# Graph network of four layers on one core: when a group's norms, roots, bounds and skip products are issued in layers 1 and 2

## The chip, the core and the metric

The kernel runs on one core of a Trainium2 chip. The metric is device time of one execution in microseconds (us); the time before is 1505.42 us, the median of three runs (1503.63 to 1510.78). The core has five engines that run beside each other, each with its own queue of instructions: TensorE (PE in the profile, its weight loads PEld), VectorE (DVE), ScalarE (ACT), GpSimd (POOL) and SyncE (SP), which here only issues DMA transfers. [...]

## What is computed

A graph of 3125 nodes with 128 features and 103125 edges goes through four layers; after each, the layer's output is added to its input and normalized over the 128 features.

```python
x = _layernorm(x + _L0_gnn_ref(...))   # weighted sum over edges, weight matrix, relu
x = _layernorm(x + _L1_gnn_ref(...))   # attention with 4 heads, and a norm of its own
x = _layernorm(x + _L2_gnn_ref(...))   # attention with one head, Q, K, V, Wo
x = _layernorm(x + _L3_gnn_ref(...))   # two mean aggregations, sigmoid
```

Layer 1 is the one that the change touches most. Its output for a node is

```python
out = sum over edges of alpha * h[src]         # alpha: softmax of leaky_relu(a_s[src] + a_d[dst])
out = out + gat_bias + x @ skip_W + skip_b
out = (out - mu) * rsqrt(var + 1e-5) * ln_g + ln_b
```

so two norms follow each other: the layer's own one, with its scale `ln_g` and shift `ln_b`, and then, with the layer's input added, the one around the layer.

## The kernel before

Nodes are padded to 25 blocks of 128. The first third of the run turns the edge list into dense count and weight matrices in DRAM. The attention of layers 1 and 2 and the sums of layer 3 are then matmuls over these matrices, with one accumulator bank in PSUM for each block of target nodes.

**Layer 1** goes over four groups of target blocks (`IG`: blocks 0 to 5, 6 to 12, 13 to 18 and 19 to 24, called groups 0 to 3 here), for each over two pairs of heads (`hp`), and for each pair over the 25 source blocks `c`. One (group, pair, c) is an *item*, 200 in all. For an item, `masks` loads a block of counts (`ct`) and makes two bf16 masks `cm`: of five masks, four come from an ACT instruction (`fm`, L1286) and a DVE one (L1287), and one from a single longer DVE instruction (L1280). `products` then issues three matmuls for each target block (L1297, L1302). Masks are made two items ahead of the products that use them. After a pair's 25 items, `sums` reads the accumulators on DVE (L1321) and combines them on POOL (L1327 to L1332); `quotients` divides and adds the result to `r` (L1337 to L1343). `r` already holds the skip product, which `skips` computes one block an item, a matmul into a spare bank (L1310) and a DVE addition (L1311).

**What follows a group.** When both pairs of heads of a group are summed, `finish1` runs its end beside the next group's items, as a chain of steps. `first_norm` takes the moments on DVE (`norm1`: L1021, L1023, L1025) and the square root on ACT (L1026). `first_scale` finishes the reciprocal on DVE and scales each block on ACT (`norm2`: L1031 to L1035), and then POOL multiplies by `ln_g`, adds `ln_b` and adds the input (L1082 to L1084). `second_norm` and `second_scale` do the same once more, into `x`. `turns` then takes the blocks one by one, two items each: `turn2` transposes the block on PE (L1044), copies it to `xT` (L537 on ACT or L539 on DVE, in turn), multiplies it for layer 2 (L1048), squares it on ACT (L1049) and copies a part to `vo` on DVE (L1050). When a half of the blocks (`QG`: 13 and 12) has been turned, `bound2` finds an upper bound for the exponents of layer 2: a maximum on DVE (L1058), `highest` (a transpose on PE, L1002, and DVE, L1004 to L1007), and an item later `spread` (PE, L1013) and a square root on ACT (L1064).

**Layer 2** goes over the two halves (`q`) and the 25 source blocks: 50 items more. `scores` makes an item's scores on PE (L1445) in banks of a pool of three (`ss`), exponentials on ACT (L1448) and a product with the counts on DVE (L1449); `products2` multiplies with `vo` (L1453). The end of layer 1's last group runs in layer 2's first items, and takes its spare banks from the same pool of three. `degrees` computes one over each node's degree for layer 3: on DVE, then a transpose on PE into such a bank (L1423), a copy on ACT (`rt`, L1425) and two DMAs.

**The order of the work.** The steps above are put off by `later(k, f)`: `f` is called at the beginning of the item that lies `k` items on (`step`). That is the order in which the program is written. The framework's scheduler then decides the order in each engine's queue: it may bring an instruction forward past others that it takes to be not ready yet, or put it back. On the chip each engine takes its queue in order, so that an instruction that waits holds all behind it. In the built program the queue of DVE around a second norm, and not the number given to `later`, says between which masks its moments stand.

Of the kernel before, what the change touches and what calls it, by code (L numbers as in the profile page):

```python
# [10 lines left out]
AF = mybir.ActivationFunctionType  # L11
# [18 lines left out]
H, C = 4, 32  # L30
# [472 lines left out]
IG = [(0, 6), (6, 7), (13, 6), (19, 6)]  # L503
# [7 lines left out]
def fast_path(  # L511
# [473 lines left out]
    def later(k, f):  # L985
        due.append((now[0] + k, f))
# [12 lines left out]
    def highest(sp, v, n):  # L999

        t = bank()
        nc.tensor.transpose(t[0:n, 0:P], v, ident)  # L1002
        m = sp.tile([P, 1], F32, name="m_all")
        nc.vector.memset(m, 0.0)  # L1004
        nc.vector.tensor_reduce(m[0:n, :], t[0:n, 0:P], AX.X, OP.max)
        d = sp.tile([P, 2 * H], F32, name="d_all")[:, 0:n]
        nc.vector.tensor_scalar(d, ident[:, 0:n], m[:, 0:1], None, OP.mult)  # L1007
        return d
# [7 lines left out]
    def norm1(sp, i, i0, n):  # L1016

        bs = sp.tile([P, 13, 6], F32, name="bs1")[:, 0:n]
        mv = sp.tile([P, 13, 2], F32, name="mv1")[:, 0:n]
        for b in range(n):  # L1020
            nc.vector.bn_stats(bs[:, b, :], i[:, i0 + b, :])  # L1021
        for b in range(n):
            nc.vector.bn_aggr(mv[:, b, :], bs[:, b, :])  # L1023
        sd = sp.tile([P, 13], F32, name="sd1")[:, 0:n]
        nc.vector.tensor_scalar(sd, mv[:, :, 1], EPS, None, OP.add)  # L1025
        nc.scalar.activation(sd, sd, AF.Sqrt)  # L1026
        return sp, mv, sd

    def norm2(state, o, i, i0, n):
        sp, mv, sd = state  # L1030
# [23 lines left out]
    def bound2(sp, q):  # L1054

        i0, n = QG[q]
        mq = sp.tile([P, 1], F32, name="mq")
        nc.vector.tensor_reduce(mq, nq[:, i0 : i0 + n], AX.X, OP.max)  # L1058
        d = highest(sp, mq, 1)

        def rest():
            mm = sp.tile([P, 1], F32, name="mm")
            spread(d, 1, mm)
            nc.scalar.activation(mm, mm, AF.Sqrt)  # L1064
            nc.vector.tensor_scalar(nm[:, q : q + 1], mm, -1.0001, None, OP.mult)

        later(1, rest)

    def finish1(sp, g, gap):

        i0, n = IG[g]
        rs = r[:, i0 : i0 + n, :]
        xs = x[:, i0 : i0 + n, :]
        keep = {}

        def first_norm():
            keep["a"] = norm1(sp, r, i0, n)
            later(gap[0], first_scale)

        def first_scale():  # L1080
            norm2(keep["a"], r, r, i0, n)
            nc.gpsimd.tensor_tensor(rs, rs, g_row[:, None, :].to_broadcast([P, n, P]), OP.mult)  # L1082
            nc.gpsimd.tensor_tensor(rs, rs, b_row[:, None, :].to_broadcast([P, n, P]), OP.add)
            nc.gpsimd.tensor_tensor(rs, rs, xs, OP.add)  # L1084
            later(gap[1], second_norm)

        def second_norm():
            keep["b"] = norm1(sp, r, i0, n)
            later(gap[0], second_scale)

        def second_scale():
            norm2(keep["b"], x, r, i0, n)
            nc.gpsimd.memset(vo[:, i0 : i0 + n, P : P + 1], 1.0)
            later(gap[0], lambda: turns(0))

        def turns(j):
            if j < n:
                one, two = turn2(sp, i0 + j)
                one()
                later(1, two)  # L1100
                later(2, lambda: turns(j + 1))
            else:
                nc.gpsimd.tensor_tensor(xs, xs, xs, OP.add)
                for q, (a, m) in enumerate(QG):
                    if i0 < a + m <= i0 + n:
                        later(1, lambda q=q: bound2(sp, q))

        first_norm()

    with ExitStack() as st:  # L1110
# [204 lines left out]
        def sums(acc, g, hp):  # L1315

            i0, n = IG[g]
            pool = lp if (g, hp) == (len(IG) - 1, H - 2) else sp
            nz = pool.tile([P, 7, 2, PW], F32, name="nz")[:, 0:n]
            for k in range(n):  # L1320
                nc.vector.tensor_reduce(  # L1321
                    nz[:, k], acc[k][:, 0 : 2 * HW].rearrange("p (h s c) -> p h c s", s=3, c=PW), AX.X, OP.add
                )
            hi = nz[:, :, :, 0:F1]
            lo = nz[:, :, :, F1 : 2 * F1]
            fbb = [fb[:, s, i0 : i0 + n, hp : hp + 2, None].to_broadcast([P, n, 2, F1]) for s in range(2)]
            nc.gpsimd.tensor_tensor(lo, lo, fbb[1], OP.mult)  # L1327
            nc.gpsimd.tensor_tensor(hi, hi, fbb[0], OP.mult)
            nc.gpsimd.tensor_tensor(hi, hi, lo, OP.add)
            nc.gpsimd.tensor_tensor(hi, hi, self_[:, i0 : i0 + n, hp : hp + 2, :], OP.add)  # L1330
            if hp == 0:
                nc.gpsimd.tensor_copy(deg[:, i0 : i0 + n], nz[:, :, 0, 2 * F1])  # L1332
            last = pool is lp

            def quotients():
                rz = pool.tile([P, 7, 2], F32, name="rz")[:, 0:n]
                nc.vector.tensor_scalar(rz, hi[:, :, :, C], 1e-38, None, OP.max)  # L1337
                nc.vector.reciprocal(rz, rz)
                nc.gpsimd.tensor_tensor(
                    hi[:, :, :, 0:C], hi[:, :, :, 0:C], rz[:, :, :, None].to_broadcast([P, n, 2, C]), OP.mult  # L1340
                )
                rh = r[:, i0 : i0 + n, hp * C : (hp + 2) * C].rearrange("p b (h c) -> p b h c", c=C)
                nc.gpsimd.tensor_tensor(rh, rh, hi[:, :, :, 0:C], OP.add)  # L1343
                if hp == H - 2:
                    later(1 if last else 3, lambda: finish1(ends[-1], g, (1, 1) if last else (1, 5)))

            later(1 if last else 4 if g else 7, quotients)

# [2 lines left out]
        for x_, (g, hp, c) in enumerate(items):  # L1351
            i0, n = IG[g]
            if (g, hp, c) == (1, 0, 0):
                zero.close()
                ap = st.enter_context(tc.tile_pool(name="f_ap1", bufs=1, space=PSUM))
                turn = [0]

                def few():

                    turn[0] ^= len(acc) < 7  # L1360
                    return ap.tile([P, 512], F32, name="acc1_6" if turn[0] else "few")

                spare.append(few)
            if c == 0:
                if g == 0:
                    acc = [zps.tile([P, 512], F32, name="acc1", tag=f"acc{k}") for k in (3, 4, 2)]
                    acc += [zpp.tile([P, 512], F32, name="acc1", tag=k) for k in ("tr_sa", "left0", "left1")]
                else:
                    acc = [ap.tile([P, 512], F32, name=f"acc1_{k}") for k in range(n)]
            if c == (2 if g else 0) and hp == (0 if g else H - 2):  # L1370
                later(0, lambda: skips(i0, i0 + n))
            if (g, hp, c) == (0, 2, 5):
                later(0, in_range)
            step()
            if g == 0 and hp == 0 and ready < NB and ready <= c + 4:
                values(ready)
                ready += 2
            for y_ in range(x_ if x_ == 0 else x_ + 2, min(x_ + 3, len(items))):
                masks(*items[y_])
            if c < NB - 2:  # L1380
                for k in range(n):
                    products(acc, g, hp, c, k)
            elif c == NB - 1:
                for k in range(n):
                    products(acc, g, hp, NB - 2, k)
                    products(acc, g, hp, NB - 1, k)
                sums(acc, g, hp)
# [15 lines left out]
    with ExitStack() as st:  # L1403
# [55 lines left out]
        def finish2(q):  # L1459

            i0, n = QG[q]
            halves = [(i0, n // 2), (i0 + n // 2, n - n // 2)]
            keep = {}

            def one(h):
                keep[h] = norm1(ends[-1], r, *halves[h])
                later(1, lambda: two(h))

            def two(h):
                norm2(keep[h], x, r, *halves[h])  # L1470
                if h == 0:
                    later(1, lambda: one(1))
                elif q == 0:
                    for g in range(3):
                        later(1 + g, lambda g=g: ips.update({g: in_parts(cp, g, x[:, 4 * g : 4 * g + 4, :])}))

            if q == 0:
                later(1, lambda: one(0))
            else:
                layer_norm(l2, x, r, QG[q])  # L1480
# [5 lines left out]
        for x_, (q, c) in enumerate(items):  # L1486
# [1 line left out]
            if c == 0:  # L1488
                acc = [ap.tile([P, 512], F32, name=f"acc2_{k}") for k in range((n + 2) // 3)]
            step()  # L1490
            if (q, c) == (0, 3):
                degrees()
            if (q, c) == (1, 12):
                for b in range(2):
# [290 lines left out]
```

## Time and profile before

The profiled execution took 1509.73 us, its span 1507.9 us; the median of the three runs is 1505.42 us. PE is busy for 92% of the span. A busy PE is not PE at its pace, since matmuls are pipelined and their ends modelled; so the number of matmuls that start in a stretch is read as well.

| stretch, us | stage | PE busy | DVE busy | ACT busy | POOL busy | granted clock |
|---|---|---|---|---|---|---|
| 541 to 950 | layer 1, items | 369.76 of 409 | 348.18 | 321.99 | 94.22 | 0.97 |
| 640 to 746 | items of group 1, end of group 0 | 95.96 of 106 | 86.93 | 82.00 | 25.01 | 0.98 |
| 746 to 848 | items of group 2, end of group 1 | 89.26 of 102 | 85.65 | 76.96 | 24.46 | 0.97 |
| 848 to 946 | items of group 3, end of group 2 | 91.19 of 98 | 81.67 | 72.38 | 25.00 | 0.97 |
| 950 to 1232 | layer 2, items | 277.50 of 282 | 128.86 | 142.29 | 15.80 | 0.99 |

The granted clock is the share of TensorE's full clock that the chip let through. "Idle before" in the views of the profile is time in which an engine had nothing running, and the name behind it says what ended that time.

### The profile page before, as it was taken

Reading aid. Unit: us, or ns where it says so; the run is one execution under the profiler, and the core shown is the slowest. Engines: PE = TensorE matmul, PEld = TensorE weight load, DVE = VectorE, ACT = ScalarE, POOL = GpSimd, SP = SyncE. Lnnn points to the kernel's source line nnn. Section 1 sums busy time; section 2 is a strip of 40 time slices with the busy share of each in tenths; the row PEclk is TensorE's granted clock in tenths of the full one; section 3 lists DMA queues with packets and bytes.
Section 4 is the critical chain, followed back from the end, with each engine's and each line's share of the span. In section 5 each row is a group of like instructions: output and inputs, shape, how many; then the busy total and the mean of one; then the engine's idle time right before and its main releaser. Section 6 shows DMA issues by size and latency. Waiting matters only on the chain.

```text
span 1507.9 us, 35015 instructions
## 1 busy us (share of the span) xinstructions
PE 1394.0 (92%) x14762; PEld 1225.2 (81%) x14775; DVE 981.9 (65%) x1621; ACT 908.5 (60%) x1857; POOL 129.5 (9%) x164
## 2 busy tenths in 40 slices
PE   3889999999998988988979989899999999999995
PEld 3889999999998877987978989677777774458995
DVE  4989899999991389887888879544464351012006
ACT  2978789888882489877777787454465331023003
POOL 1000000000000023132032113200000000000000
PEclk8999999999999999999999999999999999999998
DMA  7378788989887733433534534332222218513641
GB/s 206 94 184 229 194 221 241 236 212 229 240 213 223 230 115 114 138 106 107 142 83 116 143 86 116 124 112 69 69 64 77 81 58 299 198 43 131 199 154 46
DMA packets 209732, 223.91 MB, mean 148 GB/s; under 512 B 72988, under 2 KB 183371, under 8 KB 209309
## 3 DMA queue, kind: packets, MB, share of 16 engines
q1 hardware_dynamic: 208780, 218.51, 50.5%
q8 instruction: 117, 1.92, 0.5%
q0 software_dynamic: 400, 1.97, 0.4%
q10 hardware_dynamic: 385, 1.11, 0.2%
q14 instruction: 50, 0.41, 0.1%
HBM read 157.19 MB, written 64.36 MB: 147 GB/s over the span
## 4 chain that ended last, share of the span: by engine, by line
PE 72%; DVE 10%; ACT 8%; DMA 5%; issue 3%; POOL 2%; SPq 0%; DVEq 0%; ACTq 0%; POOLq 0%
PE wp L919 11%; PE acc L1453 9%; PE acc L1302 9%; PE s L1445 8%; PE acc L1553 7%; PE acc L1629 6%; PE acc L820 6%; PE acc L1297 5%; PE cp L911 4%; DVE cm L1287 3%; ACT wod L882 3%; DMA cw<-wd 2%; PE left L820 2%; ACT fm L1286 1%; DVE cm L1280 1%
## 5 line engine op out<-in xcount | busy, mean ns | idle before, releaser
L1302 PE MATMUL acc<-vp,cm 128*128 128x198 bf16 x2500 | 343.3, 252 | 7.6 <-DVE cm L1287 6.5
L1297 PE MATMUL acc<-vp,ct 128*128 128x204 bf16 x1250 | 316.5, 255 | 10.2 <-DVE vp L1205 4.5
L1286 ACT ACTIVATE fm<-adr,bas 128x768 bf16<-128x768 f32 (+1 forms) x320 | 287.2, 952 | 62.2 <-DVE cm L1287 60.4
L1302 PEld LDWEIGHTS <-cm 128*128 128x128 bf16 x2500 | 235.7, 98 | 24.4 <-DVE cm L1287 8.8
L919 PE MATMUL wp<-wod,ohc 128*128 128x128 bf16 x3768 | 239.1, 220 | 6.8 <-ACT cs L924 5.0
L919 PEld LDWEIGHTS <-ohc 128*128 128x128 bf16 x3768 | 220.3, 98 | 8.3 <-issue 7.8
L876 DVE TENSOR_TENSOR wod<-ohd,w 128x4096 bf16<-128x4096 bf16 (+2 forms) x122 | 221.5, 1869 | 0.4 <-PE wp L919 0.4
L1287 DVE TENSOR_TENSOR cm<-fm,ct 128x768 bf16<-128x768 bf16 (+1 forms) x320 | 200.3, 657 | 32.1 <-PE acc L1302 16.3
L882 ACT ACTIVATE wod<-ohd,wu 128x128 bf16<-128x128 bf16 x628 | 197.9, 398 | 0.0
L1449 DVE TENSOR_TENSOR e<-e,ct 128x416 f32<-128x416 f32 (+1 forms) x175 | 108.1, 624 | 110.2 <-ACT e L1448 102.1
L1448 ACT ACTIVATE e<-s,f_nm 128x416 f32<-128x416 f32 (+1 forms) x175 | 109.5, 632 | 103.1 <-PE s L1445 95.5
L1453 PEld LDWEIGHTS acc<-self__8043,e 128*128 128x128 f32 x1250 | 148.2, 193 | 19.8 <-issue 18.9
L820 PE MATMUL acc<-f_xw,cw 128*128 128x128 f32 x1000 | 146.8, 288 | 11.1 <-DMA cw<-wd 11.1
L1453 PE MATMUL acc<-self__8043,e 128*128 128x129 f32 x1250 | 148.5, 276 | 0.0
L1445 PE MATMUL s<-yT,f_xT 128*128 128x416 f32 (+1 forms) x350 | 143.1, 545 | 4.5 <-ACT rt L1425 2.5
L820 PEld LDWEIGHTS acc<-f_xw,cw 128*128 128x128 f32 x1000 | 126.5, 196 | 11.8 <-DMA cw<-wd 11.8
L1297 PEld LDWEIGHTS <-ct 128*128 128x128 bf16 x1250 | 121.8, 98 | 4.1 <-issue 2.9
L924 ACT CAST cs<-cp 128x500 bf16<-128x500 f32 x157 | 90.6, 577 | 39.1 <-PE cp L911 39.1
L1445 PEld LDWEIGHTS s<-yT,f_xT 128*128 128x128 f32 x350 | 62.6, 192 | 55.3 <-issue 40.8
L865 DVE TENSOR_TENSOR ohd<-kd,ramp 128x4096 bf16<-128x4096 bf16 (+1 forms) x41 | 90.2, 2201 | 20.2 <-PE cp L911 18.3
L930 ACT COPY ws<-wp 128x512 f32<-128x512 f32 x157 | 90.1, 578 | 20.6 <-PE wp L919 20.3
L911 PE MATMUL cp<-ohc,ohd 128*128 128x125 bf16 x1256 | 96.0, 220 | 4.1 <-ACT ws L930 3.8
(345 smaller groups left out, 1526.3 us busy)
## 6 DMA issues: line engine op xcount, KB each, us to landing
ct<-f_ctd SPq DMA_DIRECT2D x46, 800.0 KB
wd<-ws SPq DMA_DIRECT2D x39, 896.0 KB
cw<-wd SPq DMA_DIRECT2D x50, 640.0 KB
ct<-f_ctd SPq DMA_DIRECT2D x150, 192.0 KB
f_ctd<-cs SPq DMA_DIRECT2D x20, 1000.0 KB
ct<-f_ctd SPq DMA_DIRECT2D x50, 224.0 KB
ct<-f_ctd SPq DMA_DIRECT2D x25, 416.0 KB
ct<-f_ctd SPq DMA_DIRECT2D x25, 365.2 KB
```

Source lines behind the costliest of these rows:

```text
L820: steps.append(lambda j=j, a=cw[:, j - h, :]: nc.tensor.matmul(accs[j // 4][:, j % 4, :], a, xw[:, i, :], start=False, stop=(i == NB - 1 a ...
L876: tip[s] = nc.vector.tensor_tensor(packed(f, ww), packed(ohd, ww), twos(w2[s])[:, ww], OP.mult)
L882: nc.scalar.activation(wod[2][:, BW + w, :], ohd[:, BW + w, :], AF.Copy, scale=w3[:, 1, at : at + 1])
L911: nc.tensor.matmul(cp[:, j, 0:KW], ohd[:, w, :], ohc[:, w, 0:KW], start=(j == 0 and q == 0), stop=(j == 3 and q == 1), skip_group_check=True,)
L919: made = nc.tensor.matmul(wp[:, j, :], ohc[:, w, :], wod[s][:, w, :], start=(j == 0 and q == 0 and s == 0), stop=(j == 3 and q == 1 and s ...
L1286: nc.scalar.activation(f[:, : n * P], at, AF.Relu, bias=bas[:, c, h : h + 1], scale=UP)
L1287: nc.vector.tensor_tensor(m[:, : n * P], f[:, : n * P], ct[:, : n * P], OP.min)
L1297: nc.tensor.matmul(out_(F1, PW), ct[:, k * P : (k + 1) * P], vp[:, c, hp : hp + 2, :, 2 * F1 : V1], start=(c == 0), stop=False, skip_group ...
L1302: nc.tensor.matmul(out_(0, 2 * F1)[:, j], ms[j][:, k * P : (k + 1) * P], vp[:, c, hp + j, :, 0 : 2 * F1], start=False, stop=(c == NB - 1 a ...
L1445: nc.tensor.matmul(s[:, :m], xT[:, c * P : (c + 1) * P], yT[:, i0 * P + a : i0 * P + a + m], start=True, stop=True)
L1448: nc.scalar.activation(e[:, a : a + m], s[:, :m], AF.Exp, bias=nm[:, q : q + 1], scale=scale)
L1453: nc.tensor.matmul(acc[k // 3][:, (k % 3) * (P + 1) : (k % 3 + 1) * (P + 1)], es[q, c][:, k * P : (k + 1) * P], vo[:, c, 0 : P + 1], start ...
```

## The change

In `norm1` the square root is taken out and becomes a step of its own, `root`, one or two items behind the moments. The steps of `finish1` get other distances: for groups 0 to 2 the root comes two items behind the moments and the scaling one more (before: scaling one item behind), the second moments nine items behind the first scaling (before: five), and the turns four items behind the second scaling (before: one). The last group, which ends in layer 2, gets one item more between moments and scaling. `bound2` of the first half now has three steps, three items apart; that of the second half keeps two. For groups 1 to 3 the skip products begin at the item of source block 5 and not 2. In layer 2 `degrees` moves from source block 3 to 16, and the two norms behind the first half get the separate root too. No computation is added or left out.

```diff
@@ norm1
-        nc.scalar.activation(sd, sd, AF.Sqrt)
         return sp, mv, sd
+
+    def root(state):
+        nc.scalar.activation(state[2], state[2], AF.Sqrt)
@@ bound2
-        d = highest(sp, mq, 1)
-
-        def rest():
+        wait = 1 if q else 3
+
+        def rest(d):
...
-        later(1, rest)
+        def over():
+            d = highest(sp, mq, 1)
+            later(wait, lambda: rest(d))
+
+        if q:
+            over()
+        else:
+            later(wait, over)
@@ finish1
             keep["a"] = norm1(sp, r, i0, n)
-            later(gap[0], first_scale)
+            later(gap[0], lambda: root(keep["a"]))
+            later(gap[0] + 1, first_scale)
...
             keep["b"] = norm1(sp, r, i0, n)
-            later(gap[0], second_scale)
+            later(gap[0], lambda: root(keep["b"]))
+            later(gap[0] + 1, second_scale)
...
-            later(gap[0], lambda: turns(0))
+            later(1 if g == len(IG) - 1 else 4, lambda: turns(0))
@@ sums
-                    later(1 if last else 3, lambda: finish1(ends[-1], g, (1, 1) if last else (1, 5)))
+                    later(1 if last else 3, lambda: finish1(ends[-1], g, (1, 2) if last else (2, 9)))
@@ items of layer 1
-            if c == (2 if g else 0) and hp == (0 if g else H - 2):
+            if c == (5 if g else 0) and hp == (0 if g else H - 2):
                 later(0, lambda: skips(i0, i0 + n))
@@ finish2
                 keep[h] = norm1(ends[-1], r, *halves[h])
-                later(1, lambda: two(h))
+                later(1, lambda: root(keep[h]))
+                later(2, lambda: two(h))
@@ items of layer 2
-            if (q, c) == (0, 3):
+            if (q, c) == (0, 16):
                 degrees()
```

## The prediction

> **What bounds the kernel now.** I read the page first, then in layers 1 and 2 the waits of PE, the starts of matmuls by stretch, and the timelines of the engines around the worst stretches.
>
> ```profile
> PE 1394.0 (92%) x14762; PEld 1225.2 (81%) x14775; DVE 981.9 (65%) x1621; ACT 908.5 (60%) x1857; POOL 129.5 (9%) x164
> ```
>
> PE bounds the kernel, so only time in which PE stands still or runs slowly can be won. The change touches 600 to 1240 us. The waits of PE from 640 to 950 us (us in total, times, longest):
>
> ```profile
> PE acc L1302 <- DVE cm L1287: 6.5, 6, 3.2
> PE acc L1044 <- ACT f_x L1035: 6.0, 1, 6.0
> PE few L1310 <- DVE f_xw L1311: 5.2, 5, 2.3
> PE few L1044 <- DVE self__8043 L1050: 4.8, 2, 2.5
> PE few L1002 <- DVE mq L1058: 1.5, 1, 1.5
> PE acc L1013 <- DVE d_all L1007: 1.5, 1, 1.5
> ```
>
> In order: masks that come late, the first turn waiting for the second scaling, skip products waiting for their bank, turns waiting for theirs, and the two halves of the bound. All PE waits there come to some 30 us of 310. Slow running is seen in starts by stretch (busy PE, starts, granted clock, DMA):
>
> ```profile
> 680.00:700.00 20.00, 16.64 (x156) 0.91 0.42 122
> ...
> 720.00:750.00 30.00, 30.00 (x345) 1.00 0.51 142
> ...
> 772.00:796.00 24.00, 16.29 (x157) 0.86 0.26 71
> ...
> 872.00:894.00 22.00, 17.71 (x163) 0.84 0.29 78
> ```
>
> Undisturbed, 345 matmuls start in 30 us: 0.087 us each, so an item of 18 takes 1.57 us and one of 21 takes 1.83 us. From 772 to 796 only 157 start where 276 could. Layer 2 has hardly a stall after 985 us (PE busy 277.5 of 282). The worst stretch, on DVE, POOL and ACT:
>
> ```profile
> 776.19 4.14 DVE L1287 TENSOR_TENSOR cm<-fm,ct 128x768 bf16<-128x768 bf16 x2 [1.24 <-ACT fm L1286]
> 782.31 1.46 DVE L1021 BATCH_NORM_STATS2 bs<-f_xw 128x6 f32<-128x128 f32 x7 [1.98 <-POOL f_xw L1084]
> ```
> ```profile
> 777.64 2.27 POOL L1083 TENSOR_TENSOR f_xw<-f_xw,f_b_row 128x896 f32<-128x896 f32 x1
> 779.99 2.29 POOL L1084 TENSOR_TENSOR f_xw<-f_xw,f_x 128x896 f32<-128x896 f32 x1
> ```
> ```profile
> 785.25 0.21 ACT L1026 ACTIVATE sd<-sd 128x7 f32<-128x7 f32 x1 [3.96 <-DVE sd L1025]
> ...
> 787.38 2.79 ACT L1035 ACTIVATE f_x<-f_xw,ms,sd 128x128 f32<-128x128 f32 x7
> ```
>
> ACT scales, POOL takes three operations, DVE stands 1.98 us before the second moments with the next masks queued behind them, ACT stands 3.96 us at the root with masks behind it, and PE stands until 787.9 because a transpose of the scaled `x` is next in its queue.
>
> **The bound of the first half.** Both waits lie on PE (1.5 and 1.5 us). Three items between the steps, some 4.7 us, are more than either wait. Nothing is added. Gain 2.7; ends 2 and 3.
>
> **Roots and turns.** In the built queues the turns of groups 0 to 2 stand about 20 masks (10 items) later; the root and the second scaling also stand behind more masks, and the scalings are mixed with `fm` instead of six or seven in a row (7 x 0.40 = 2.8 us in the last row above).
> - Group 1: the 6.0 us wait for `f_x` goes. What is late next is a mask. At 781.8 us DVE has finished 230 masks of this layer's count, enough for one item more on PE (1.57, to 783.4). The new DVE queue has five of the seven moments ahead of the next mask: 782.3 + 5 x 0.21 = 783.4, then masks of 0.95 and 0.5 us, so PE goes on at 784.9 and two items later is where it is at 787.9 now, or a little ahead. It gains about two items and 0.9 us: 4 us; ends 2 (masks stay late for some items) and 6.
> - Group 0: its waits for the turns' bank are 2.5 us at 689.3 (DVE's copy waits 2.29 us for ACT's square, behind 9.4 us of `fm` that the six scalings had held up) and 2.3 us at 711 (DVE's copy behind six sums, 2.98 us). The turns now start after that pair's sums. The first wait goes, with 0.8 us at 684 for `f_xT`. Of the second, 1 us comes back as late masks. Gain 4; ends 2.5 and 5.5.
> - Group 2: a wait of 0.9 us for `f_x` goes. Gain 0.9.
> - The cost: the turns of groups 1 and 2 now begin just behind the sums of a pair. For group 1 the first copy to `xT` is DVE's, behind six sums and two masks that run beside POOL (1.2 to 1.3 us each). PE meets its matmul one item after the sums, some 2.6 us before the copy is done; a late mask would take 0.7 of it anyway. Cost 1.8; ends 0 and 3. In group 2 the first copy is ACT's and hidden.
>
> **The second moments.** Nine items instead of five read like 6 us more for POOL. But the scheduler brings the moments forward: in DVE's queue those of group 1 still start behind mask 230 (seven before; five, then two between masks after), of group 2 behind mask 328 in both, of group 0 behind 128 instead of 126. So the waits for POOL stay (1.7, 2.0 and 3.6 us), and with them the 3.2 us mask wait on PE in group 2. In group 0 three `fm` (3 x 0.95 us) now stand between three and three first scalings on ACT. POOL's input is up to 2.8 us later while DVE has two masks (1.2 us) more ahead: 1.4 us lost, ends 0 and 2.8. Here the row and a rule agree on a limit and differ on the hope. Two masks took 4.14 us beside POOL, where 1.1 us is usual (0.56 each on either side). "SBUF — State Buffer", section "Who interferes with whom", of the Trainium skill says why: an operation with two SBUF inputs and a GpSimd operation that reads SBUF exclude each other whole, the second waits. So filling the 2.0 us wait before L1084's end with masks, if the moments did move, would give by plain durations 2.0/0.56 = three masks, by the rule one at most (0.6 us). I take the rule: even a real move is worth little, and I count nothing.
>
> **The skips.** Groups 1 to 3 lose 5.2 us at L1310, since each needs DVE to be some three items ahead. Three items later DVE has had about 3 x 0.4 us to recover (a mask pair costs 75% of a PE item: DVE busy is 22.6 of 30 us in 720 to 750), but the first norm's moments, 2.5 us of DVE, now stand ahead of most skips. Gain 2; ends -1 and 5.
>
> **Layer 2.** PE waits 2.54 us for `rt`:
>
> ```profile
> 979.26 1.72 PE L1445 MATMUL s<-yT,f_xT 128*128 128x416 f32 x2 [2.54 <-ACT rt L1425]
> ```
> ```profile
> 977.56 1.28 ACT L1026 ACT_TABLE_LOAD   x1 [4.61 <-DVE sd L1025]
> ...
> 980.09 1.28 ACT L1448 ACT_TABLE_LOAD   x1
> 981.39 1.60 ACT L1448 ACTIVATE e<-s,f_nm 128x416 f32<-128x416 f32 x3
> ```
>
> `degrees` leaves this place, but ACT's queue here is unchanged: root, one scaling, then exponentials. With the third bank free PE makes one score and one product more and then stands at the fourth score until the first exponential, 981.9 us. It saves one product and one transpose, 0.4 us; ends -1.5 (a longer single stand, slow clock behind it) and 3.5. At source block 16 `rt` stands among exponentials with ACT half idle, and its two DMAs pass thirteen loads of `ct2` on SP: they hold that queue for a landing, hidden by the loads' lead of an item (5.6 us). The later root, scaling and turns of group 3 end at item 220, the second bound at 223, ahead of their uses at 224 and behind: 0. In the second half the norms move two items in a stretch where PE never waits: 0. Table loads stay the same in number.
>
> **The clock.** After the 2.5 us wait at 689.26 a matmul pair takes 0.54 us instead of 0.34 for 3 us: 1.5 us lost. After those at 787.9 and 882.8 the granted clock of the stretch falls to 0.86 and 0.84. "TensorE: Matmul & The Clock Gate", "HAM oscillation", has it that gaps over about 3.4 us bring the half clock; the row has it after 2.5. By the rule only the 6.0 us stall costs, 1.5 us won; by the rows two of the three go: 3. I take 2, between them, since about 2 us of stand remain in group 1.
>
> **Sum.** -2.7 - 4 - 4 - 0.9 + 1.8 + 1.4 - 2 - 0.4 - 2 = -12.8. On the profiled 1509.7 that gives 1496.9; the median of the runs is 4.3 lower, and on it the forecast is 1493 us.
>
> **Rivals.**
> - *DVE's deficit returns* (24%). DVE is busy 254 of 306 us in 640 to 946 and at 9.9 of 10 in many slices after the sums. A PE wait that goes then comes back as a late mask. For it: 6.5 us are mask waits already. Against it: DVE stands for PE some 20 us there, just after the turns' waits (2.7 us at 693). Left are the bound and a third of the turns: -4 to -5, 1501.
> - *POOL's input is late and holds the masks* (13%). One mechanism: the first scalings, split on ACT, reach POOL later, and the moments keep their place in DVE's queue. Group 0 +2.8, group 2 +0.9 (one `fm` more); each stand then outlasts the two items of masks in hand, so 1.5 us of half clock follow twice; the turns behind sums cost 2.6 in two groups; the skips gain nothing and masks take the turns' gains: 2.8 + 0.9 + 3 + 5.2 - 2.7 = +9, 1514. It decides once DVE's wait for POOL passes the masks' lead of about 3.5 us; in group 2 it is 3.6 already.
> - *The change doesn't do what it says* for the second moments; that is in the sum.
>
> **Chances and range.** The forecast has 63%. Within 0.5% (7.5 us, about what a measurement here can tell from none) lie the second case and the weak edge of the forecast, less its own strong edge: faster 0.61, same 0.27, slower 0.12. The ends of the terms reach from about 0 to 27 us of gain; a range of 1483 to 1506 leaves out the slower rival and the strongest gains.
>
> **What will show it.** Right: no PE wait for L1002, L1013 or, in layer 1, for `f_x`; no wait for L1050 near 690; DVE still waiting for L1084 three times by 2 us or more; a PE wait of 3 to 4 us for an exponential near 980. Wrong: waits for masks (L1298 then) rising above 12 us in all, L1310's waits not below 5 us, or a new stand behind the sums above 3 us.

## The result, and the profile after

Over 20 runs of each kernel the changed one took 1508.87 us (median; 1502.47 to 1514.41), the one before 1508.27 us (1503.63 to 1511.98). The ratio is 1.0006 with a 95% interval of 0.9995 to 1.0016: no difference that can be measured, where 1493 us was forecast. The forecast stood on a median of three runs (1505.42 us); on the median of all 20 its gain of 12.8 us would give 1495.5. The profiled execution has a span of 1505.8 us (1507.9 before). Layer 1 began 3.1 us earlier, at 536.9 us, and no part of the change runs ahead of it; layer 2 took 1.3 us more. In this part of the code the line numbers of the changed kernel are 2 (norms) to 11 (layer 1 and behind) higher.

| | layer 1, us | of it PE stands | of it slow | layer 2, us |
|---|---|---|---|---|
| before | 409.6 | 42.4 | 6.5 | 288.5 |
| after | 409.6 | 39.4 | 10.0 | 289.9 |
| after, once more | 412.4 | 41.5 | 10.2 | 289.9 |

Layer 1 is counted here from its first product to the first product of layer 2, and layer 2 from there to its last product. "Stands" is the sum of PE's idle times above 50 ns. "Slow" is worked out from the starts of the mask and count products: they follow each other after 0.087 us in undisturbed stretches; where one follows another after 0.115 to 0.215 us, what is above 0.087 is summed. Take both away, and 360.2 to 360.8 us are left in each row: the change left the work as it was and moved only stands and slow stretches.

The equal lengths hide losses and gains. Counted from the first product of each group to that of the next, the items of group 0, which the change doesn't touch, took 1.6 us more, those of group 1 2.5 us more, those of group 2 3.1 us less and those of group 3 1.0 us less (once more: 1.4 more, 3.9 more, 3.2 less, 0.7 more). The end of a group runs beside the next group's items, so the largest loss lies at the end of group 0, where 4 us were to be won.

PE's waits in the changed kernel, 640 to 950 us (us in total, times, longest):

```profile
PE acc L1308 <- DVE nz L1332: 7.5, 3, 4.0
PE few L1321 <- DVE f_xw L1322: 5.2, 3, 3.8
PE acc L1313 <- DVE cm L1298: 4.0, 5, 2.1
PE acc L1313 <- DVE cm L1291: 2.9, 2, 2.3
PE acc L1050 <- DVE f_xT L539: 2.0, 1, 2.0
PE few L1050 <- DVE f_xT L539: 1.7, 1, 1.7
```

The waits for `f_x` (6.0 us), for the bound (3.0) and for the turns' bank near 690 us are gone, as forecast. At the top stands a wait that was 1.0 us before: 7.5 us for `nz`, the sums at the end of a pair of heads, which must be read before the accumulators can be used again. Starts by stretch (PE busy and starts stand first, the granted clock third from the right) beside the slow stretches of before:

```profile
690.00:710.00 20.00, 15.87 (x158) 14.79 (x156) 14.80 (x22) 12.19 (x13) 6.30 (x5) 0.91 0.47 155
...
769.00:793.00 24.00, 20.69 (x211) 19.41 (x209) 21.61 (x56) 18.82 (x29) 6.89 (x3) 0.93 0.34 90
...
869.00:891.00 22.00, 19.67 (x202) 18.88 (x202) 17.40 (x45) 17.16 (x27) 5.64 (x3) 0.92 0.35 94
```

The ends of groups 1 and 2 became better (211 starts in 24 us where there were 157, and 202 in 22 where there were 163). The end of group 0 did not: it merely stands ten microseconds later. SP's queue and DVE tell why. First SP in 680 to 700 us (start, length, line, operation):

```profile
681.52 2.16 SPq L1285 DMA_DIRECT2D ct<-f_ctd  x2
688.92 0.37 SPq L1279 DMA_DIRECT2D adr<-add__8057  x1
689.38 5.78 SPq L1285 DMA_DIRECT2D ct<-f_ctd  x6
```

After the `ct` load at 683.4 us SP issues nothing for 5.5 us. It stands at `adr`, the row that every partition gets for the masks of a pair (128x2x768 fp32, 786 KB), here for the pair after the next. That load fills the buffer of the pair that is just ending, so it waits for that pair's last masks, and the `ct` loads of the next items are queued behind it. SP's waits at this load between 600 and 900 us, for the masks that DVE makes alone (`cm`) and for `fm`, first before and then after:

```profile
SPq L1268 <- DVE cm L1280: 5.7, 4, 3.1
SPq L1268 <- ACT junk L1049: 2.2, 1, 2.2
SPq L1268 <- ACT fm L1286: 0.5, 2, 0.3
```
```profile
SPq L1279 <- ACT fm L1297: 6.0, 3, 2.9
SPq L1279 <- DVE cm L1291: 4.8, 4, 2.3
```

The last `fm` is late on ACT, because the six scalings of the second norm now stand among the masks of the pair's last items:

```profile
682.98 1.96 ACT L1297 ACTIVATE fm<-adr,bas 128x896 bf16<-128x896 f32 x2
684.84 1.25 ACT L1037 ACTIVATE f_x<-f_xw,ms,sd 128x128 f32<-128x128 f32 x3
```

At this pair the stand is not new. Before, the six scalings stood in one row ahead of the pair's last ten `fm`, and the load went out 5.4 us after the `ct` load ahead of it, when the tenth `fm` had ended at 688.6 us (the row above names `junk`, which ended just behind it):

```profile
676.89 2.41 ACT L1035 ACTIVATE f_x<-f_xw,ms,sd 128x128 f32<-128x128 f32 x6
679.21 9.43 ACT L1286 ACTIVATE fm<-adr,bas 128x896 bf16<-128x896 f32 x10
```
```profile
681.30 2.27 SPq L1274 DMA_DIRECT2D ct<-f_ctd  x2
688.66 0.37 SPq L1268 DMA_DIRECT2D adr<-add__8057  x1
```

It cost nothing there, since PE was standing for the turns itself, 2.5 us at 689.3. The change took that stand away, and PE came to the end of the pair ahead of the blocks.

On DVE, in the changed kernel, the first masks of the new pair and then the sums follow (last column: idle before, and who ended it):

```profile
694.43 1.16 DVE L1298 TENSOR_TENSOR cm<-fm,ct 128x896 bf16<-128x896 bf16 x2 [4.88 <-PE acc L1308]
696.36 0.62 DVE L1298 TENSOR_TENSOR cm<-fm,ct 128x896 bf16<-128x896 bf16 x1 [0.77 <-DMA ct<-f_ctd]
696.90 1.15 DVE L1291 SCALAR_TENSOR_TENSOR cm<-adr,nas,ct 128x896 bf16<-128x896 f32 x1
697.96 3.47 DVE L1332 TENSOR_REDUCE nz<-acc 128x134 f32<-128x402 f32 x7
```

DVE stands idle for 4.88 us and 0.77 us for blocks of counts that have not landed, with the sums queued behind these masks. (The first of these rows names PE. But the load of the block that this mask reads, issued at 689.38 us, had its last part land at 694.31 us; and below, with the load of `adr` moved, the same masks run long before PE's last product of the pair.) PE waits 4.0 us for the sums. At 805 us, the end of group 2's first pair, it happens again: SP stands from 794.8 to 797.7 us, DVE stands 3.2 us for a block, and PE waits 2.6 us. Here the stand is new: the load went out 3.2 us after the `ct` load ahead of it, where it was 0.6 us before.

### The profile page after: what moved, and what is told of

It is laid out like the page before. It is cut to its first block, busy times and chain, and to the rows that moved or that the text cites. A ratio compares the mean times of both kernels' runs of the same rounds, so it can differ in the third digit from the quotient of the medians.

```text
span 1505.8 us, 35044 instructions
## 1 busy us (share of the span) xinstructions
PE 1394.0 (93%) x14775; PEld 1224.8 (81%) x14775; DVE 983.4 (65%) x1621; ACT 908.3 (60%) x1857; POOL 129.9 (9%) x164
## 4 chain that ended last, share of the span: by engine, by line
PE 71%; DVE 11%; ACT 8%; DMA 4%; issue 2%; POOL 2%; SPq 0%; DVEq 0%; ACTq 0%; POOLq 0%
PE wp L919 10%; PE acc L1464 9%; PE acc L1313 9%; PE s L1456 8%; PE acc L1565 7%; PE acc L1641 6%; PE acc L820 6%; PE acc L1308 4%; PE cp L911 3%; DVE cm L1298 3%; ACT wod L882 3%; PE left L820 2%; DMA cw<-wd 2%; DVE cm L1291 1%; ACT fm L1297 1%
## 5 line engine op out<-in xcount | busy, mean ns | idle before, releaser
L1313 PE MATMUL acc<-vp,cm 128*128 128x198 bf16 x2500 | 347.6, 253 | 8.2 <-DVE cm L1298 4.0
L1298 DVE TENSOR_TENSOR cm<-fm,ct 128x768 bf16<-128x768 bf16 (+1 forms) x320 | 203.9, 665 | 32.5 <-PE acc L1313 13.4
```

Of the source, the lines that this page charges most:

```text
L1298: nc.vector.tensor_tensor(m[:, : n * P], f[:, : n * P], ct[:, : n * P], OP.min)
L1313: nc.tensor.matmul(out_(0, 2 * F1)[:, j], ms[j][:, k * P : (k + 1) * P], vp[:, c, hp + j, :, 0 : 2 * F1], start=False, stop=(c == NB - 1 a ...
```

## The experiments

Two theories were held against each other. **Loads:** what the moved steps win is lost at the ends of pairs, since late scalings hold the last `fm`, that holds the `adr` load, and that holds the next `ct` loads. **DVE:** DVE has no time to spare, so a wait that goes returns as a late mask whatever the loads do. What the slow stretches behind a stand do was read from the traces beside them. Times are given as the ratio to the kernel before on the same chip, with the 95% interval, and in us of about 1507.

**The bound alone**, in the kernel before:

```diff
-        d = highest(sp, mq, 1)
-        def rest():
+        wait = 1 if q else 3
+        def rest(d):
...
-        later(1, rest)
+        def over():
+            d = highest(sp, mq, 1)
+            later(wait, lambda: rest(d))
...
```

> The kernel before with only the first half's bound in three steps. Layer 1 (its first product to the first product of layer 2) takes 409.6 us before and with the whole change. As predicted: both PE waits of the bound go and layer 1 takes 407. Theory DVE (DVE has no time to spare, so what PE does not wait for here it waits for at the next mask or sum): the waits go and layer 1 takes 409 to 410. Theory loads (the block loads that come late at the end of a head pair set the pace, and a gain ahead of them is lost there): the bound lies in the last third of group 2's first pair, ahead of a pair's end, so 408 to 410, with a longer wait for the sums at that pair's end, near 805 us.

Measured: 0.9972 (0.9960 to 0.9985), 4 us faster; layer 1 took 407.0 us, as predicted (stands 40.7, slow 5.4). Both waits went. By itself this part is worth about what it was priced at; that the length fits so closely is partly luck, since stands fell by 1.7 us (a turn's copy now keeps PE 1.2 us at 802 us) and slow products by 1.1.

**The steps alone** (separate roots, other distances, later turns), in the kernel before:

```diff
-            later(gap[0], first_scale)
+            later(gap[0], lambda: root(keep["a"]))
+            later(gap[0] + 1, first_scale)
...
-            later(gap[0], lambda: turns(0))
+            later(1 if g == len(IG) - 1 else 4, lambda: turns(0))
...
-    finish1(ends[-1], g, (1, 1) if last else (1, 5))
+    finish1(ends[-1], g, (1, 2) if last else (2, 9))
```

> The kernel before with only the steps behind a group's norms (separate roots, second moments nine items behind, turns four items behind), in layers 1 and 2; bound, skips and degrees as before. The prediction's terms for this part: -4 -4 -0.9 +1.8 +1.4 and -2 of clock: layer 1 takes 402. Theories loads and DVE: the waits of the turns go and come back at the ends of pairs (PE waits for the sums, 7 us and more in all) and at xT: 409 to 411.

Measured: 0.9997 (0.9987 to 1.0007); layer 1 408.5 us (stands 38.2, slow 9.8). So the waits came back, as both theories against the prediction had it. PE's row for `nz` is there without the bound's or the skips' edit:

```profile
PE acc L1301 <- DVE nz L1325: 7.8, 4, 4.4
```

This run shows one thing more. The two halves of the first bound, which waited 1.5 us each before, stand without any wait here, though `bound2` is as it was:

```profile
839.92 0.27 PE L1002 MATMUL few<-f_ident,mq 128*1 128x128 f32 x1
...
841.98 0.35 PE L1013 MATMUL acc<-d_all,ones 128*128 128x1 f32 x2
```

Where the later turns put it, DVE is ready in time. The steps and the bound remove the same two waits. The prediction counted these waits once, under the bound, and did not see that the steps end them too.

**The load of the broadcast row moved**: in the changed kernel, and as a control in the kernel before, `adr` is queued on SP ten `ct` loads ahead of its first use, when its buffer has long been free.

```diff
-                nc.sync.dma_start(adr[:, :, : n * P], ...)
+                with ExitStack() as held:
+                    if len(loads) > 10:
+                        held.enter_context(tc.issue_after(loads[-10].ins))
+                    nc.sync.dma_start(adr[:, :, : n * P], ...)
...
-            nc.sync.dma_start(ct[:, : n * P], ...)
+            loads.append(nc.sync.dma_start(ct[:, : n * P], ...))
```

> The changed kernel with the load of a pair's broadcast row (adr) put into SP's queue ten loads ahead of its first use instead of at the end of the pair before the last. SP then does not stand there while block loads queue behind it. Theory loads: DVE's gaps of 4.9 us at 694 and 3.2 us at 803 go, PE's waits for the sums fall from 7.5 us to under 3, layer 1 takes 402 to 405. Theory DVE: the gaps go, but the masks and sums stay late since DVE has no time to spare: 408 to 410.

> The kernel before with the same edit to the load of the broadcast row alone. Theory loads: in before the late loads lie beside the turns' waits, so little is won: layer 1 takes 408 to 409.5; the change then is worth 4 us or more once the loads are out of its way. Theory DVE: 409 to 410, as e3.

Measured: in the changed kernel 0.9960 (0.9949 to 0.9972), 6 us faster than before, layer 1 403.9 us (stands 34.7, slow 8.6). In the kernel before 0.9997 (0.9984 to 1.0009), layer 1 409.9 us. The same edit is worth 6 us with the change and nothing without it: in the kernel before the late load is covered. DVE at the same place of the changed kernel with the load moved:

```profile
688.78 0.62 DVE L1302 TENSOR_TENSOR cm<-fm,ct 128x896 bf16<-128x896 bf16 x1 [0.30 <-ACT fm L1301]
...
692.12 1.15 DVE L1295 SCALAR_TENSOR_TENSOR cm<-adr,nas,ct 128x896 bf16<-128x896 f32 x1
693.19 3.47 DVE L1336 TENSOR_REDUCE nz<-acc 128x134 f32<-128x402 f32 x7
```

The idle 4.88 us are gone, masks go through as fast as ACT delivers `fm`, and PE's wait for `nz` falls from 7.5 to 1.0 us. Theory DVE, which asked for no gain, falls as the explanation of these 6 us.

**The steps alone, with the load moved:**

> The steps behind the norms alone (as in the run with the steps alone, whose layer 1 took 408.5 us) together with the load of the broadcast row ten loads ahead of its use. Theory loads: the steps' gain was covered by the late loads, so layer 1 takes 403 to 405, where the load's edit alone gave 409.9. Theory bound (the bound's three steps carry most of what the full change wins with the load moved): 407 to 408.5.

Measured: 0.9952 (0.9934 to 0.9971), 7 us faster, where the steps without the load and the load without the steps both gave 0.9997. So the steps' gain exists and was covered. Layer 1 was even shorter than expected, 401.3 us; its stands are 36.2 us, 5.4 less than with the load alone, and the rest is the clock: behind its first twelve items this execution has 0.05 us of slow products, although it has stands of 2.0 and 2.3 us for a mask. That part need not be the edit's (see the last section). Theory bound falls too: this run lacks the bound's edit and is not slower than the run that has all.

**Turns four items later still** (the distance 4 becomes 8), load moved:

> The changed kernel with the load moved (layer 1 403.9 us there) and the turns of groups 0 to 2 eight items behind the second scaling instead of four, clear of a pair's sums. As the prediction had it, the turns right behind the sums cost PE waits for xT (1.9, 1.5 and 2.2 us for the first of them, 0.9 us for each of two banks): if these come from the sums that stand before the copies in DVE's queue, they go and layer 1 takes 399 to 401. If a copy is late wherever the turns stand, since DVE and ACT have masks queued ahead of it, 403 to 404.5.

Measured: 0.9950 (0.9936 to 0.9965); layer 1 401.9 us. The waits for `xT` fell from 5.0 to 2.6 us, but stands in all are 35.0 us against 34.7: mask and skip waits rose by 2.8 us. The 2 us in layer 1's length are slow products (5.6 against 8.6). Here theory DVE is right: a wait for a copy went and came back at masks and skips.

**Skips at source block 2 again**, load moved, and **skips at 5 alone**, in the kernel before:

```diff
-            if c == (5 if g else 0) and hp == (0 if g else H - 2):
+            if c == (2 if g else 0) and hp == (0 if g else H - 2):
```

> The changed kernel with the load moved, and the skip products of groups 1 to 3 at source block 2 again instead of 5. PE waits 7.5 us for their bank's addition with 5. If the later start is worth the 2 us that were predicted: layer 1 takes 406. If the single stand of 3.8 us at 655 only takes the place of the waits of 2.5 and 0.9 before: 403.5 to 404.5. If the later start costs: 402.

> The kernel before with only the skip products of groups 1 to 3 at source block 5. As predicted -2: layer 1 takes 407.6. If one stand of about 4 us takes the place of several (as with the whole change): 409.5 to 411.

Measured: with the skips back at 2, 0.9942 (0.9926 to 0.9959) and layer 1 402.3 us against 403.9; alone in the kernel before, 1.0010 (0.9997 to 1.0023) and 411.1 us against 409.6. No gain either way. Of the 1.6 and 1.5 us by which the lengths differ, 1.2 each are slow products in the layer's first twelve items, ahead of the edit, so a loss isn't shown either. Skips alone, in 655 to 662 us:

```profile
656.77 0.80 PE L1310 MATMUL few<-f_l_swt,f_xT 128*128 128x128 f32 x2 [3.90 <-DVE f_xw L1311]
```

Started at block 2, group 1's skips wait 2.3 and 0.7 us there; started at 5 they meet the first norm's moments in DVE's queue and wait 3.9 us in one piece.

**The second moments held**: in DVE's queue they are put behind the last mask that is written before them, so that "nine items" really moves them (behind masks 148, 242 and 342 of the layer, not 128, 230 and 328).

```diff
+            with tc.issue_after(latest[0].ins):
                 keep["b"] = norm1(sp, r, i0, n)
```

> The changed kernel with the load moved, and the second moments held in DVE's queue behind the masks that are written before them, so that they really stand later (behind masks 148, 242 and 342 of the layer instead of 128, 230 and 328). If DVE's waits for GpSimd (1.7, 2.0 and 3.6 us) are what makes the masks late, the mask waits of PE at 781 and 873 us (2.8 and 2.7 us) go: layer 1 takes 398 to 400. If the masks that now run beside GpSimd take as long as the wait did (two masks took 4.14 us there), 402.5 to 404.

> The changed kernel with the second moments held behind the masks, and the load of the broadcast row left where it was. With that load moved, holding them won 8.5 us of layer 1 (403.9 to 395.4). If the late block loads cover this gain too: layer 1 takes 406 to 409.6. If the two lie in different stretches (loads at the ends of pairs, moments in the middle of them): 401 to 403.

Measured: with the load moved 0.9922 (0.9905 to 0.9940), 12 us faster than before, layer 1 395.4 us (stands 32.9, slow 3.0). With the load where it was 0.9956 (0.9940 to 0.9973), 7 us faster, layer 1 398.7 us (34.3 and 4.2), better than either outcome expected. DVE of the first of them, where the changed kernel stands 1.98 us for GpSimd and then takes moments:

```profile
770.68 4.38 DVE L1304 TENSOR_TENSOR cm<-fm,ct 128x768 bf16<-128x768 bf16 x2 [0.34 <-ACT fm L1303]
774.98 2.83 DVE L1297 SCALAR_TENSOR_TENSOR cm<-adr,nas,ct 128x768 bf16<-128x768 f32 x1
777.74 1.95 DVE L1304 TENSOR_TENSOR cm<-fm,ct 128x768 bf16<-128x768 bf16 x4
```

The mask beside GpSimd takes 2.83 us instead of 1.0: it ends with GpSimd's operation (777.0 us) and 0.8 us. So filling the wait gives one mask, no more. But within 9 us of the first row seven masks are made, where with the moments in front of them (only the load moved) it was four. PE's stand of 2.3 us falls to 1.1 us, and no slow products follow it.

With the moments held and the load not moved, the second scaling of group 0 falls behind the end of the pair, and SP's row changes to

```profile
SPq L1281 <- ACT fm L1299: 0.3, 1, 0.3
```

from 6.0 us; PE's waits for `nz` are 2.5 us instead of 7.5. That closes the chain from the other end: without any edit to the loads, they come in time once no scaling stands in front of the pair's last `fm`.

**The changed kernel again:**

> The changed kernel once more, for how far the lengths of the stages repeat. Layer 1 took 409.6 us and layer 2 289.9; if a stage's length is set by the order of the queues alone, both come within 0.5 us, and only the part before layer 1 (536.9 us) moves by some us.

Measured: layer 2 289.9 us, as expected; layer 1 412.4, not within 0.5 us. The items of groups 1 and 3 take 1.4 and 1.7 us longer, with 2.1 us more of stands in all. A difference in layer 1 of some 3 us between two single traces therefore says little; ratios and waits carry the verdicts above.

**All four edits together:**

> The changed kernel with four edits together: the load of the broadcast row moved, the second moments held, the turns eight items behind the second scaling, the skip products at source block 2 again. Alone each won 5.7, 8.5, 2.0 and 1.6 us of layer 1. If they add up: 391.8 us. If the stalls hide behind each other: 393 to 396. In all 1490 to 1495 us.

Measured: 1492.58 us (1490.16 to 1494.53), 0.9907 (0.9889 to 0.9924): 14 us faster than before. Layer 1 took 394.0 us (stands 29.7, slow 4.3), so the gains overlap in part. It beats both kernels.

## Why the prediction was wrong

- **The turns of groups 0 and 1, -4 each: the step that failed.** It priced the waits that go, and next to them looked only for late masks on DVE. It read on ACT that the six scalings had held up 9.4 us of `fm`, but never followed SP's queue in layer 1, where the `adr` load waits for the last of these `fm`, with the next blocks behind it. At the end of group 0 that load was late before too, covered by the very stand of 2.5 us that was to be won; in group 2 the moved scalings made it late. SP stood 5.5 and 3.2 us, and PE 4.0 and 2.6 us for the sums. Steps alone: 0.9997; with that load out of the way: 0.9952. One line was misread as well: PE's stand at 711 us is put down to a copy behind six sums of 2.98 us. The sums were seven, 3.47 us, and over at 702.5 us. The square that this copy waits for was done at 708.6 us, and the copy, at 710.7, stood behind masks, one of which took 1.98 us beside GpSimd.
- **The second moments.** That the scheduler keeps their place was right, and DVE's three waits for GpSimd stayed (1.7, 2.0 and 3.6 us). But "even a real move is worth little" was wrong: it counted the masks that fit into the wait. By "Who interferes with whom" of "SBUF — State Buffer" in the Trainium skill a DVE instruction with two SBUF inputs and a GpSimd one that reads SBUF exclude each other; so only one mask fits, and the run agrees (2.83 us for it). The move is worth 6 us with the load moved, by the ratios 0.9960 and 0.9922. What goes with it in the trace is the moments ahead of the next masks, and half of PE's stand with the slow products behind it; how much is due to each was not tried apart.
- **The bound, -2.7.** Right alone (layer 1 -2.6). Beside the steps its edit adds nothing that can be told, since they end the same waits: with the load moved and the skips at 2, 0.9952 without it and 0.9942 with it (and with `degrees` later), and the intervals overlap. These waits stand once in the sum, so counting them twice is not the error.
- **The turns behind the sums, +1.8.** Too small: the waits for `xT` come to 4.4 us in three groups, and group 2's, called hidden, is one of the longest with 2.0.
- **The skips, -2.** Wrong; no gain is seen (ratio alone 1.0010). The term's own doubt, moments in front of most skips, is what happened.
- **Layer 2, -0.4.** The forecast stand for the exponential is there, 3.9 us. Layer 2 took 1.3 us more, inside the term's bounds.
- **The clock, -2.** Slow products rose from 6.5 to 10.0 us instead. 1.4 of that lies in the first twelve items, where nothing was changed. The rest lies behind stands: before, three of 2.5 to 6.0 us were followed by slow products, after, five of 2.1 to 4.0 us.
- **The rivals.** "DVE's deficit returns" had the change nearest (-4 to -5 us, against +0.6), but by another mechanism: where most was lost, DVE stood idle for 4.88 us. It holds only for the turns that were moved further on. "POOL's input is late" did not happen: DVE's three waits for POOL are as long as before (7.3 us in all), though two of its items came true, the skips and the turns behind sums.

Part by part against the sign list: all four signs of "right" are in the trace (the first of DVE's three waits at 1.7 us), and of "wrong" there are two: the skips' waits for `few` are 5.2 us as before, not below 5, and a stand of more than 3 us is new at a pair's sums. That sign was meant for the turns behind the sums, where PE stands 2.0 us at most; the 4.0 us are for the sums themselves. So most of the waits that were looked at went as told, and the loss lay in a queue that was not.

## What to carry to other kernels

When steps are moved, follow the queue of the engine that only issues loads as well: a load that reuses a buffer waits for the last reader of that buffer, and everything queued behind it is late with it, so the reader's place in its queue is the price. Where another stand covers such a late load, taking that stand away wins little until the load moves too. A distance in the program is worth nothing until the built queue shows it; where the scheduler undoes it, an order put in by hand gave what the distance was meant to give. And of two edits that end the same wait the second is worth little or nothing: price it with the first already in.

## What was not expected of the hardware

Whether slow products follow a stand is partly chance. In the changed kernel, traced twice, PE stands 2.29 us for the same mask of group 2, until 784.9 and 785.5 us. Six microseconds around (PE busy and starts, then the granted clock), first trace and second:

```profile
784.00:790.00 6.00, 4.97 (x39) 0.72 0.16 45
```
```profile
784.60:790.60 6.00, 4.90 (x54) 1.00 0.25 68
```

Two kernels of this study that differ in layer 1's skips alone have the same stand of 3.85 us at the same place in layer 2. With the skips at 5 the next 18 products take 4.07 us and the granted clock of the ten microseconds around is 0.77:

```profile
973.65 1.76 PE L1460 MATMUL s<-yT,f_xT 128*128 128x416 f32 x2 [3.85 <-ACT e L1463]
975.20 4.07 PE L1468 MATMUL acc<-self__8043,e 128*128 128x129 f32 x18
```

With the skips at 2 they take 2.17 us at a clock of 1.00:

```profile
972.55 0.97 PE L1460 MATMUL s<-yT,f_xT 128*128 128x416 f32 x2 [3.85 <-ACT e L1463]
973.36 2.17 PE L1468 MATMUL acc<-self__8043,e 128*128 128x129 f32 x18
```

Layer 2 took 290.9 and 288.2 us in them. Over all traces here the slow products of layer 1 range from 2.7 to 10.2 us, and its first twelve items alone have 1.3 to 2.8 us of them in kernels that do not differ there. What sets the chance was not tried. It is one reason why lengths of single traces say less than the ratios.
